# Deformable convolution from weight tables: table writes moved to other queues and paced by patch, loads issued in parts, the image without border columns, tents by a second ACT pass, five product buffers

## The chip, the cores and the metric

The kernel runs on one NeuronCore of a Trainium2 chip, from one launch. The metric is device time in microseconds. TensorE (PE) multiplies matrices, VectorE (DVE) and ScalarE (ACT) work elementwise, GpSimd (POOL) does small jobs, and SyncE (SP) only issues DMAs. SP, ACT and POOL each issue DMAs in the order of their own instruction stream.

## The reference

Two layers on x of shape (8, 128, 64, 64), float32:

```python
# layer 0
v = gn(x)                                   # group norm, 32 groups
om = conv3x3(v, off_w) + off_b              # 27 channels: 18 offsets, 9 masks
# for each of the 9 taps: sample v bilinearly at the tap's place plus its offset,
# times sigmoid(mask); then a sum over taps and channels with w
y = einsum('bckhw,ock->bohw', val, w) + b
x = x + relu(batchnorm(y) * gamma + beta)   # statistics over all 8 images
# layer 1
v = gn(x)
# gate on the pooled v: two of four experts; their 3x3 kernels are mixed per image
x = x + conv3x3(v, mixed) + conv3x3(v, shared_w) + biases
```

## The kernel before, in words

Layer 0 is `dense()`. Offsets here are below 2 in size, so bilinear sampling is written as a product of two tent functions, one along rows and one along columns, each with five shifts (`NR`). A second path, `general()`, is branched over when all offsets are that small.

An image is cut into patches of 8 x 16 pixels, which are the 128 partitions of a matmul. A block is four patches below each other (`t`); an image has eight blocks and 32 patches (`i`). For each patch and each row of taps `ky`:

- `z_part`: one matmul (L425) of the patch's pixels (`xh`) with the weights of three taps gives z in PSUM, and ACT copies it to SBUF (L431). It is emitted one patch ahead.
- `weights`: VectorE multiplies an x tent and a y tent, `x_wts` and `y_wts`, into the product s (L443), one patch ahead, in a pool `ap4` of four buffers.
- `s_part`: three matmuls (L464) of z with s add into `py`, an accumulator with a halo for two patches; `collect` (L481) adds it to the image's half `y` on VectorE. `end_half` takes statistics of y and stores it (L504).

The tents come from two tables per image in DRAM, `y_table` and `x_table` (taby, tabx in the trace). `load_ty` reads the y tents of two patches by eight DMAs on SP into one of three buffers, `load_tx` the x tents of a block by sixteen DMAs on POOL (L393) into one of two buffers. Each broadcasts rows over partitions.

The generator `tables(b + 1)` builds the next image's tables beside the current image. Its steps end in `yield`, and the patch loop calls it: twice after the first tap row, once after the second and third. In order: `repack` of the current image's second half (ACT, L222), loading of x into `pad` (ACT, L243; `pad` is 66 x 66 with zero borders), statistics (VectorE, L257), group norm (a pow on POOL, L277, and ACT, L283), the offset convolution (L310), evacuation twice, once row by row and once column by column (L292, L295), writing both to DRAM (rowwise on ACT, L323; colwise on SP, L327), reading them back with image rows and columns on partitions (`off`, `mask`, on SP, L339 to L341), the sigmoid (L343), the tents (ACT takes absolute values, L348; VectorE clips them, L351, and multiplies by the mask, L352), and the table writes: for each tap and half two y writes on ACT (L360) and one x write on SP (L369). An x write is 64 partitions x 5 shifts x 35 elements of 4 bytes, that is 320 runs of 140 bytes.

`pause(n)` puts n empty yields between steps. The order is written out by hand: each engine runs its instructions in the order of emission. So an instruction that waits holds all behind it on its engine, DMA issues included. Five patches before the image's end what is left of `tables` is emitted at once, and `repack` of the next image follows.

```python
for _ in range(2 if ky == 0 else 1):
    next(made, None)
```

Layer 1 follows (L810 on): per image a residual with gate and an ordinary 3 x 3 convolution (L887). The change does not touch it.

Of the kernel before, what the change touches and what calls it, by code (L numbers as in the profile page):

```python
# [16 lines left out]
P = 128  # L17
# [40 lines left out]
def deform_moe_conv(  # L58
# [122 lines left out]
    def dense():  # L181

        with ExitStack() as st:
# [3 lines left out]
            a3 = st.enter_context(tc.tile_pool(name="d3", bufs=3))  # L187
            ap4 = st.enter_context(tc.tile_pool(name="d4", bufs=4))
            ps_c = st.enter_context(tc.tile_pool(name="ps_c", bufs=2, space=PSUM))
# [4 lines left out]
            nc.gpsimd.memset(zeros, 0.0)  # L194
            pad = padded(a1, "pad")
            offw_sb = a1.tile([P, TAPS, 32], F32, name="offw_sb")
# [20 lines left out]
            def repack(b, h):  # L217

                xh[b, h] = a2.tile([P, NRB // 2, NCB, PC, PR], F32, name="xh")
                for r in range(NRB // 2):  # L220
                    r0 = 1 + PR * (h * NRB // 2 + r)
                    nc.scalar.copy(  # L222
                        xh[b, h][:, r].rearrange("p c x y -> p y c x"),
                        pad[:, r0 : r0 + PR, 1 : W + 1].rearrange("p y (c x) -> p y c x", c=NCB),
                    )
                    yield

            def tables(b):
# [12 lines left out]
                for q in range(4):  # L241
                    rows = slice(16 * q, 16 * q + 16)
                    nc.scalar.dma_start(  # L243
                        out=pad[:, 1 + 16 * q : 17 + 16 * q, 1 : W + 1],
                        in_=x[b].rearrange("c (h w) -> c h w", w=W)[:, rows],
                    )
                if b < 2:
                    for t in tables_of:
                        nc.sync.dma_start(
                            out=t[b].rearrange("(p a n) -> p a n", p=P, n=256),  # L250
                            in_=zeros.unsqueeze(1).to_broadcast([P, fill, 256]),
                        )
                yield from pause(8)
                stats = small.tile([P, NCH, 6], F32, name="stats")
                part = [pad[:, 1 + 8 * c : 9 + 8 * c, 1 : W + 1] for c in range(NCH)]
                for c in range(NCH):
# [45 lines left out]
                for c in range(2):  # L302
                    pc = ps_c.tile([P, CH], F32, name="pc")
                    for k in range(TAPS):
                        ky, kx = divmod(k, 3)
                        if k == LATER and done:
                            evacuate(*done.pop())
                        for j in range(4):
                            r = 16 * j + 8 * c + ky
                            nc.tensor.matmul(  # L310
                                pc[32 * j : 32 * j + 32],
                                lhsT=offw_sb[:, k, :],
                                rhs=pad[:, r : r + 8, kx : kx + W],
                                start=(k == 0),
                                stop=(k == TAPS - 1),
                            )
                        yield
                    done.append((c, pc))
# [3 lines left out]
                for j in range(4):  # L322
                    nc.scalar.dma_start(  # L323
                        out=rowwise[b][:, j * HW // 4 : (j + 1) * HW // 4],
                        in_=omr[32 * j : 32 * j + 27],
                    )
                    nc.sync.dma_start(  # L327
                        out=colwise[b][:, :, H // 4 * j : H // 4 * (j + 1)],
                        in_=omc[32 * j + 9 : 32 * j + 18],
                    )  # L330
                nc.vector.tensor_reduce(
                    most[:, b : b + 1], omr, AX.X, ALU.max, apply_absolute_value=True
                )
                yield from pause(LATER)

                off = a1.tile([P, TAPS, W], F32, name="off")
                mask = a1.tile([H, TAPS, W], F32, name="mask")
                rows = rowwise[b].rearrange("s (h w) -> h s w", w=W)
                nc.sync.dma_start(out=off[0:H], in_=rows[:, 0:9, :])  # L339
                nc.sync.dma_start(out=off[H:P], in_=colwise[b].rearrange("s w h -> w s h"))  # L340
                nc.sync.dma_start(out=mask, in_=rows[:, 18:27, :])  # L341
                yield from pause(LATER)
                nc.scalar.activation(mask, mask, AF.Sigmoid)  # L343
                tent = a1.tile([P, NR, TAPS, W], F32, name="tent", tag="om")
                for i in range(NR + 1):

                    if i < NR:
                        nc.scalar.activation(tent[:, i], off, AF.Abs, bias=steps[:, i : i + 1])  # L348
                    if i:
                        t = tent[:, i - 1]  # L350
                        nc.vector.tensor_scalar(t, t, 1.0, 1.0, ALU.min, ALU.subtract)  # L351
                        nc.vector.tensor_tensor(t[0:H], t[0:H], mask, ALU.mult)  # L352
                    yield
                for k in range(TAPS):
                    ky, kx = divmod(k, 3)
                    for h in range(2):
                        for c in (2 * h, 2 * h + 1):
# [10 lines left out]
                        first = (h * NQI + kx) * NR * HSTEP + (NR - 1) * HSTEP + k * HROWS  # L368
                        nc.sync.dma_start(  # L369
                            out=bass.AP(  # L370
# [14 lines left out]

            def load_tx(t):
                if t >= len(blocks):
                    return
                b, h, c = blocks[t]
                flat = x_wts[t % 2].rearrange("p a b c -> p (a b c)")  # L390
                for qx in range(PC):
                    src = x_table[b][h, PC * c + qx + ROWPAD]
# [4 lines left out]

            def load_ty(u):

# [4 lines left out]
                flat = y_wts[u % 3].rearrange("p j a b c -> p j (a b c)")  # L404
                for qy in range(PR):
                    q = PR * (h * NRB // 2 + r) + qy + ROWPAD
# [89 lines left out]
            def end_half(b, h):  # L496
# [3 lines left out]
                for g in range(first * W // CH, last * W // CH):  # L500
                    at = g * CH - first * W
                    nc.vector.bn_stats(ystats[:, b * NCH + g, :], y[:, at : at + CH])
                    yield
                nc.scalar.dma_start(out=ydram[b][:, first * W : last * W], in_=y)  # L504

# [3 lines left out]
            for _ in tables(0):  # L509
                pass  # L510
            for u in range(2):
                load_ty(u)
                load_tx(u)
            for _ in repack(0, 0):
# [5 lines left out]
            for i, (t, r) in enumerate(patches):  # L520
# [6 lines left out]
                if at == per_image - 5:  # L527
                    for _ in made:
                        pass
                    if b + 1 < B:  # L530
                        made = repack(b + 1, 0)
                if i % 2 == 1:
                    load_ty(i // 2 + 2)
                if r == NRB // 2 - 1:
                    load_tx(t + 2)
                if i % 2 == 0:
                    py = ps_y.tile([P, UR + PR, UC], F32, name="py")
                for ky in range(3):
                    weights(i + 1, ky)
                    s_part(i, ky, py)  # L540
                    z_part(i + 1, ky)
                    for _ in range(2 if ky == 0 else 1):
                        next(made, None)
                    next(ended, None)
# [402 lines left out]
```

## Time and profile before

| what | value |
|---|---|
| median of 3 runs | 2686.2 us (2680.69 to 2688.17) |
| profiled execution, own time | 2694.36 us |
| its span, first to last instruction | 2692.6 us |
| mean granted TensorE clock | 0.897 |
| PE / DVE / ACT / POOL busy | 80% / 58% / 24% / 24% |
| DMA | 355,130 packets, 289.39 MB |
| of these under 512 B | 290,256 packets |

Times in a profile are of one execution. Views used further on: the page with its groups of instructions by line; stretches of the span with the busy time of each engine, the granted clock and the mean busy share of the 16 DMA engines; waits, with what ended them; and the timeline. A name with a small q (SPq, ACTq) is an engine's queue that issues DMAs; "ywts<-taby" is a DMA from the y table into the y tents' buffer. A number in brackets at a timeline row's end is idle time of the engine before it, and what ended it. A gap of an engine that nobody waits for costs nothing.

### The profile page before, as it was taken

How to read it: one execution, taken by the hardware profiler on the slowest of the kernel's cores; microseconds unless marked ns; L12 is line 12 of the kernel's file. 1: busy time of each engine (PE TensorE's matmuls, PEld its weight loads, DVE VectorE, ACT ScalarE, POOL GpSimd, SP SyncE). 2: the span in 40 equal slices, each digit the busy share in tenths (PEclk: the TensorE clock that was granted, in tenths of full speed). 3: DMA queues.
4: the chain of work that ended last, by engine and by line, in shares of the span. 5: the costliest groups of instructions: out<-in, count | busy, mean ns of one | idle time of the engine just before them, and what ended most of it. 6: DMA issues, size and time to landing. Idle time of an engine off the chain costs nothing. (4 is left out here: it accounts for less than half of the span.)

```text
span 2692.6 us, 25651 instructions
## 1 busy us (share of the span) xinstructions
PE 2163.6 (80%) x8530; PEld 1446.2 (54%) x8530; DVE 1550.2 (58%) x1520; ACT 641.0 (24%) x1114; POOL 657.4 (24%) x1141
## 2 busy tenths in 40 slices
PE   3188698759877796689688958895899569999999
PEld 1065575547555665565466636664778424444444
DVE  1075586648665866586577646765798653333321
ACT  2132142213221322132222212221232131111110
POOL 3222132223122322132222222222234142112200
PEclk8599898889898998789798968896999879999999
DMA  3963584396447734873576367635766352222200
GB/s 89 81 161 74 95 168 100 82 103 155 89 87 116 170 70 92 110 159 68 104 119 152 75 90 117 146 75 93 128 149 142 127 181 94 98 94 98 80 34 35
DMA packets 355130, 289.39 MB, mean 107 GB/s; under 512 B 290256, under 2 KB 294352, under 8 KB 353840
## 3 DMA queue, kind: packets, MB, share of 16 engines
q1 hardware_dynamic: 155952, 187.42, 32.2%
q0 software_dynamic: 32768, 56.13, 10.7%
q10 hardware_dynamic: 166272, 44.12, 9.0%
q8 instruction: 71, 1.16, 0.2%
q14 instruction: 67, 0.55, 0.1%
HBM read 231.54 MB, written 55.92 MB: 107 GB/s over the span
## 5 line engine op out<-in xcount | busy, mean ns | idle before, releaser
L443 DVE TENSOR_TENSOR s<-xwts,ywts 128x684 f32<-128x684 f32 (+6 forms) x768 | 1169.4, 1560 | 523.9 <-DMA ywts<-taby 138.2
L464 PE MATMUL py<-s,z 128*128 128x240 f32 (+10 forms) x4608 | 1073.1, 372 | 334.9 <-DVE s L443 239.1
L464 PEld LDWEIGHTS py<-s,z 128*128 128x128 f32 x4608 | 888.2, 203 | 659.8 <-issue 296.2
L393 POOL DMA_DIRECT2D xwts<-tabx x1024 | 526.0, 519 | 1378.3 <-DVE s L443 1114.4
L425 PE MATMUL pz<-dw_sb,xh 128*128 128x384 f32 x1536 | 658.1, 512 | 67.3 <-ACT xh L222 67.3
L431 ACT COPY z<-pz 128x384 f32<-128x384 f32 x768 | 367.5, 481 | 1383.0 <-PE pz L425 1121.6
L887 PE MATMUL pc<-pad,wmix 128*128 128x512 f32 x1152 | 504.1, 598 | 10.7 <-ACT x L826 10.7
L887 PEld LDWEIGHTS pc<-pad,wmix 128*128 128x128 f32 x1152 | 217.2, 190 | 278.1 <-issue 267.4
L425 PEld LDWEIGHTS pz<-dw_sb,xh 128*128 128x128 f32 x1536 | 302.3, 201 | 79.6 <-ACT xh L222 68.2
L895 DVE SCALAR_TENSOR_TENSOR x<-pc,bmix,x 128x512 f32<-128x512 f32 x64 | 47.9, 748 | 321.1 <-PE pc L887 321.1
L310 PE MATMUL pc<-pad,offw_sb 128*32 128x512 f32 x1152 | 155.8, 606 | 9.0 <-ACT pad L283 9.0
L876 ACT ACTIVATE pad<-x,shift,scale 128x512 f32<-128x512 f32 x64 | 51.5, 814 | 329.5 <-PE pc L887 324.8
L827 POOL TENSOR_TENSOR x<-x,xt 128x512 f32<-128x512 f32 x64 | 96.3, 1529 | 54.7 <-ACT x L826 29.4
L481 DVE TENSOR_TENSOR y<-py,y 128x418 f32<-128x418 f32 (+2 forms) x128 | 75.4, 589 | 49.4 <-PE py L464 48.5
L310 PEld LDWEIGHTS pc<-pad,offw_sb 128*32 128x32 f32 x1152 | 32.1, 109 | 96.2 <-issue 72.7
L222 ACT COPY xh<-pad 128x512 f32<-128x512 f32 x64 | 69.5, 1146 | 49.0 <-DMA taby<-tent 49.0
L351 DVE TENSOR_SCALAR tent<-tent 128x576 f32<-128x576 f32 x40 | 17.9, 448 | 97.2 <-ACT tent L348 61.5
L111 POOL TENSOR_TENSOR scale<-ve,nhalf 128x1 f32<-128x1 f32 x8 | 4.4, 547 | 271.2 <-DVE ve L110 271.2
L828 DVE BATCH_NORM_STATS2 stats<-x 128x6 f32<-128x512 f32 x64 | 42.8, 686 | 32.9 <-POOL x L827 25.1
L826 ACT ACTIVATE x<-x,yshift,yscale 128x512 f32<-128x512 f32 x64 | 47.0, 802 | 53.7 <-DMA x<-yd 53.7
L283 ACT ACTIVATE pad<-pad,shift,scale 128x512 f32<-128x512 f32 x64 | 47.6, 809 | 17.1 <-DVE shift L280 17.1
L263 PE MATMUL pm<-mv,gsel 128*128 128x1 f32 x16 | 4.7, 360 | 58.5 <-DVE mv L261 58.5
(85 smaller groups left out, 388.6 us busy)
## 6 DMA issues: line engine op xcount, KB each, us to landing
ywts<-taby SPq DMA_DIRECT2D x1024, 112.5 KB
xwts<-tabx POOLq DMA_DIRECT2D x1024, 53.4 KB, 5.3
pad<-in_x_dram ACTq DMA_DIRECT2D x32, 512.0 KB
xt<-in_x_dram SPq DMA_DIRECT2D x32, 512.0 KB
x<-yd SPq DMA_DIRECT2D x32, 512.0 KB
out_dram<-x SPq DMA_DIRECT2D x64, 256.0 KB
yd<-y ACTq DMA_DIRECT2D x8, 1280.0 KB
tabx<-tent SPq DMA_DIRECT2D x144, 43.8 KB
```

The source lines that it names most:

```text
L222: nc.scalar.copy(xh[b, h][:, r].rearrange("p c x y -> p y c x"), pad[:, r0 : r0 + PR, 1 : W + 1].rearrange("p y (c x) -> p y c x", c=NCB),)
L310: nc.tensor.matmul(pc[32 * j : 32 * j + 32], lhsT=offw_sb[:, k, :], rhs=pad[:, r : r + 8, kx : kx + W], start=(k == 0), stop=(k == TAPS - 1),)
L393: nc.gpsimd.dma_start(out=flat[qx * PR : (qx + 1) * PR, qx * HSTEP : (qx + NR) * HSTEP], in_=src.unsqueeze(0).to_broadcast([PR, NR * HSTEP]),)
L425: nc.tensor.matmul(pz, lhsT=xh[b, h][:, r, c].rearrange("p x y -> p (x y)"), rhs=dw_sb[:, 3 * ky * P : 3 * (ky + 1) * P], start=True, stop ...
L431: nc.scalar.copy(zs[i][:, 3 * ky * P : 3 * (ky + 1) * P], pz)
L443: nc.vector.tensor_tensor(s[:, :, lo:hi, cl:ch], x_wts[t % 2][:, cl:ch, 3 * ky : 3 * ky + 3, first + lo : first + hi].rearrange("p c k r - ...
L464: nc.tensor.matmul(py[:, top + lo : top + hi, cl - kx + 2 : ch - kx + 2], lhsT=zs[i][:, k * P : (k + 1) * P], rhs=s[:, kx, lo:hi, cl:ch], ...
L481: nc.vector.tensor_tensor(part, py[:, rl:rh, cl:ch], part, ALU.add)
L827: nc.gpsimd.tensor_tensor(y, y, xt[:, c % 2 * CH : (c % 2 + 1) * CH], ALU.add)
L876: nc.scalar.activation(pad2[:, 1 + 8 * c : 9 + 8 * c, 1 : W + 1], x1[:, c * CH : (c + 1) * CH].rearrange("p (h w) -> p h w", w=W), AF.Iden ...
L887: nc.tensor.matmul(pc, lhsT=wmix[:, k, :], rhs=pad2[:, 8 * c + ky : 8 * c + ky + 8, kx : kx + W], start=(k == 0), stop=(k == TAPS - 1),)
L895: nc.vector.scalar_tensor_tensor(y, pc, bmix, y, ALU.add, ALU.add)
```

## The change

- `pad` has no border columns (66 rows x 64). Each load is then contiguous per partition. The offset convolution takes the middle taps first; a side tap multiplies 63 of 64 columns.
- A yield follows each of the four loads of x.
- The colwise writes and the three reloads move from SP to ACT; the x table's writes move from SP to POOL. In the patch loop SP issues y loads alone (and, for the first two images, the zero filling of the tables).
- Two waits of `LATER` (4) yields around the reloads become 6, and one of 8 becomes 6. The generator is called three times in an even patch and four times in an odd one, instead of four times in each.
- Tents: ACT takes the absolute value and then relu(1 - t) in a second pass in place; VectorE only multiplies by the mask.
- `load_ty` of a patch pair is issued in two halves of four, in two patches following each other, one patch pair earlier. `load_tx` is issued in parts of 6, 6 and 4 over three patches of the block before.
- `end_half` stores y in pieces of 512 columns.
- The product pool has five buffers instead of four.

```diff
-            ap4 = st.enter_context(tc.tile_pool(name="d4", bufs=4))
+            ap4 = st.enter_context(tc.tile_pool(name="d4", bufs=5))
...
-            pad = padded(a1, "pad")
+            pad = a1.tile([P, HP, W], F32, name="pad")
...
                     nc.scalar.dma_start(
-                        out=pad[:, 1 + 16 * q : 17 + 16 * q, 1 : W + 1],
+                        out=pad[:, 1 + 16 * q : 17 + 16 * q],
                         in_=x[b].rearrange("c (h w) -> c h w", w=W)[:, rows],
                     )
+                    yield
...
-                yield from pause(8)
+                yield from pause(6)
...
-                    for k in range(TAPS):
+                    for n, k in enumerate((1, 4, 7, 0, 3, 6, 2, 5, 8)):
                         ky, kx = divmod(k, 3)
+                        lo, hi = max(0, 1 - kx), min(W, W + 1 - kx)
...
-                                rhs=pad[:, r : r + 8, kx : kx + W],
+                                rhs=pad[:, r : r + 8, lo + kx - 1 : hi + kx - 1],
...
-                    nc.sync.dma_start(
+                    nc.scalar.dma_start(
                         out=colwise[b][:, :, H // 4 * j : H // 4 * (j + 1)],
...
-                yield from pause(LATER)
+                yield from pause(6)
...
-                nc.sync.dma_start(out=off[0:H], in_=rows[:, 0:9, :])
-                nc.sync.dma_start(out=off[H:P], in_=colwise[b].rearrange("s w h -> w s h"))
-                nc.sync.dma_start(out=mask, in_=rows[:, 18:27, :])
-                yield from pause(LATER)
+                nc.scalar.dma_start(out=off[0:H], in_=rows[:, 0:9, :])
+                nc.scalar.dma_start(out=off[H:P], in_=colwise[b].rearrange("s w h -> w s h"))
+                nc.scalar.dma_start(out=mask, in_=rows[:, 18:27, :])
+                yield from pause(6)
...
-                for i in range(NR + 1):
-
-                    if i < NR:
-                        nc.scalar.activation(tent[:, i], off, AF.Abs, bias=steps[:, i : i + 1])
+                for i in range(NR):
+                    t = tent[:, i]
+                    nc.scalar.activation(t, off, AF.Abs, bias=steps[:, i : i + 1])
+                    nc.scalar.activation(t, t, AF.Relu, bias=1.0, scale=-1.0)
                     if i:
-                        t = tent[:, i - 1]
-                        nc.vector.tensor_scalar(t, t, 1.0, 1.0, ALU.min, ALU.subtract)
-                        nc.vector.tensor_tensor(t[0:H], t[0:H], mask, ALU.mult)
+                        t = tent[0:H, i - 1]
+                        nc.vector.tensor_tensor(t, t, mask, ALU.mult)
                     yield
...
-                        nc.sync.dma_start(
+                        nc.gpsimd.dma_start(
                             out=bass.AP(
                                 tensor=x_table[b].tensor,
...
+                    nc.scalar.dma_start(
+                        out=ydram[b][:, g * CH : (g + 1) * CH], in_=y[:, at : at + CH]
+                    )
                     yield
-                nc.scalar.dma_start(out=ydram[b][:, first * W : last * W], in_=y)
...
-            for u in range(2):
-                load_ty(u)
-                load_tx(u)
+            load_tx(0, range(PC))
+            for u in range(3):
+                load_ty(u, range(PR if u < 2 else PR // 2))
...
-                if i % 2 == 1:
-                    load_ty(i // 2 + 2)
-                if r == NRB // 2 - 1:
-                    load_tx(t + 2)
+                load_ty((i + 1) // 2 + 2, range(PR // 2) if i % 2 else range(PR // 2, PR))
+                load_tx(t + 1, range(6 * r, min(PC, 6 * r + 6)))
...
-                    for _ in range(2 if ky == 0 else 1):
+                    next(made, None)
+                    if ky == 0 and i % 2:
                         next(made, None)
```

## The prediction

> **What bounds the kernel now.** I first read the stretches of the dense stage. The starts of the L464 matmuls in the timeline cut it into patches (18 records to a patch, 32 patches to an image). It starts at 131.3 us; images 0 to 6 take 1823.6 us together (260.5 each), image 7 takes 170.5 and layer 1 the last 567.2. Image 7 has no tables to build after it; the others build those of the next image meanwhile.
>
> ```profile
> core 0: us, PE busy (x) PEld busy (x) DVE busy (x) ACT busy (x) POOL busy (x), PEclk, DMA share, GB/s
> 647.00:904.20 257.20, 207.10 (x918) 152.23 (x917) 171.96 (x150) 67.16 (x122) 66.24 (x130) 0.89 0.57 112
> 1954.90:2125.40 170.50, 169.00 (x762) 137.83 (x762) 155.03 (x120) 52.25 (x100) 53.74 (x104) 1.00 0.53 122
> ```
>
> See two things: alone, a pass over an image is bound by TensorE (169.0 of 170.5 us, VectorE close behind with 155.0), and beside the tables TensorE idles 50 us and runs at a lower clock. Next I cut image 2 where its pace changes.
>
> ```profile
> 656.90:692.60 35.70, 23.18 (x76) 17.98 (x75) 22.30 (x24) 4.69 (x10) 8.21 (x16) 0.71 0.81 183
> 704.00:752.20 48.20, 48.20 (x265) 24.48 (x263) 26.71 (x21) 12.53 (x24) 16.47 (x32) 1.00 0.40 76
> 772.60:804.60 32.00, 13.15 (x49) 9.47 (x47) 16.61 (x22) 9.04 (x15) 5.86 (x12) 0.84 0.52 98
> 804.60:862.00 57.40, 38.68 (x144) 30.28 (x145) 28.16 (x22) 8.51 (x18) 12.21 (x24) 0.79 0.67 100
> 862.00:904.20 42.20, 42.19 (x193) 35.12 (x194) 40.67 (x32) 14.74 (x27) 17.48 (x35) 1.00 0.68 151
> ```
>
> These are patches 2-4 (image loading), 7-11 (offset convolution), 16-17 (reload of offsets, tents), 18-23 (tables written) and 24-31. The same patches of image 7 take 16.4, 27.4, 11.9, 31.8 and about 42. So image 2 pays 19.3 + 20.8 + 20.1 + 25.6 + 0 more. The 20.8 is TensorE's own work; the other 65 us are stalls, on no busy engine. The waits of ACT and of SP's queue, then the timeline, say on what.
>
> ```profile
> ACT mask L343 <- DMA mask<-rowwise: 107.3, 8, 14.6
> ACT z L431 <- DMA taby<-tent: 91.0, 31, 5.6
> SPq L407 <- DMA rowwise<-om: 244.9, 8, 37.4
> SPq L407 <- DMA taby<-tent: 218.0, 53, 15.3
> ```
> ```profile
> 783.13 0.68 ACT L343 ACTIVATE mask<-mask 64x576 f32<-64x576 f32 x1 [13.19 <-DMA mask<-rowwise]
> ```
> ```profile
> 804.95 15.94 SPq L407 DMA_DIRECT2D ywts<-taby  x8
> 821.19 7.38 SPq L369 DMA_DIRECT2D tabx<-tent  x8
> 828.68 14.41 SPq L407 DMA_DIRECT2D ywts<-taby  x8
> 843.13 5.26 SPq L369 DMA_DIRECT2D tabx<-tent  x8
> 848.50 7.21 SPq L407 DMA_DIRECT2D ywts<-taby  x8
> ```
> ```profile
> 664.82 4.08 POOL L393 DMA_DIRECT2D xwts<-tabx  x8 [14.40 <-DVE s L443]
> 671.45 0.52 POOL L393 DMA_DIRECT2D xwts<-tabx  x1 [2.56 <-DMA xwts<-tabx]
> ```
>
> ACT stands 13 us before the sigmoid, with the z copies that feed TensorE behind it. SP's y loads stand in turn behind the x table's writes, and VectorE starves. Eight DMAs go out at once, then each waits for one to land: the built program's order has eight completion semaphores for SP and ACT together, and eight for POOL.
>
> **The change, per image (0 to 6).** Floor: image 7's 170.5, plus 20.8 for the convolution (six of nine taps lose 8 of 512 columns, 0.2 us), plus VectorE's extra: 8 statistics x 0.69, 5 mask products x 0.75 and a reduction of 1.2, 10.5 us where it is nearly the bound; the buffers take some, I count 7. The two evacuations lie under the convolution. The five dropped tensor_scalar (0.45 each) give 2.2 that are already out of the 10.5. Floor 198.
>
> Contiguous image: 8,192 packets of 256 B become 512 of 4 KB. The first took 12.2 us of all 16 DMA engines; packets of 4,096 B took 0.2 us elsewhere in this trace, so 6.4 now, spread over four yields. The 10.2 us of VectorE on xwts in patches 2-4 should go. Of the stretch's 19.3, 5.5 are statistics (in the floor); of 13.8 I keep 2. Statistics and normalisation cost the same on contiguous data: 0.69 at L257 against 0.68 at L502, 0.81 at L283 against 0.80 at L826.
>
> Reload and tents: ACT now issues the four colwise writes (0.83 each), the three reloads (1.27, 0.62, 0.63) and five more passes (0.77): 9.7 us, and the y stores as eight DMAs instead of two (about 0.35 each against 0.8, 1 more). ACT's copies fill 1.44 of 5.3 us per patch, so over the five patches 15-20 this fits if it comes in pieces; TensorE runs out after about two copies, 3.5 us. Pauses rise from 4 to 6 at 3.5 yields per patch instead of 4: reloads come 9 us after the writes, the sigmoid 9 after those. Colwise landed 6 us after its last issue (771.1 to 777.2), the mask 5 after its own: the sigmoid's wait goes, the reload may wait some 3 us on ACT. What is late next is the z copy. I keep 4 of 20.1.
>
> Table stage: SP no longer has x writes, so VectorE's wait for y loads goes (they are also issued one patch pair earlier, behind nothing but weights of a patch that VectorE has left; each waits for its buffer, and only y loads queue behind). ACT remains: 7 y writes x 0.63 + 3 copies x 0.48 is 5.9 us per patch against 5.3. And the eight semaphores: before, 16 SP and ACT transfers per patch (8 y writes, 4 x writes, 4 y loads) in 9.6 us mean a turn of 4.8 us; now 11 per patch, 6.6 us at the same turn, 8.3 at 6.0. The same writes in less time load the engines more (0.67 of 57.4 us is 38 us of DMA work), so I take nearer the second: 13 of 5.1 patches' excess (7 to 15). Emission is 91 yields of the 94 there are up to patch 27, so nothing is forced out at once.
>
> POOL: 18 x writes of 320 rows, never seen on POOL here. Price c: its row for 8 rows is 0.52 us, the floor; by packets (320 to that row's 32) 5.2 is the ceiling. SP's row for the very shape is 0.62 against 0.59 for a y load of 32 rows, so the shape hardly counted there; software may count more, and I take 1.0, near the floor. From patch 21 to 27 POOL must do 18c + 20 x 0.52 and wait 5.3 us for the landing: 33.7 of 35.4 us. Cost 2; every microsecond of c above 1.1 costs 18. A gain is excluded: POOL did none of this. The next image needs the tables at patch 31 only. POOL's one pow per image (L277) waits for VectorE with x loads behind it, as before. The fifth product buffer is worth nothing by itself: VectorE's 130 us of waits for a free one happen while TensorE is the bound; it only widens the slack.
>
> Sum: 198 + 2 + 4 + 13 + 2 + 1 for the y stores = 220 against 260.5. Start-up: 36 y writes took 45.7 us sharing semaphores with SP's 18; alone 30 to 45.7, I take 6 off; extra passes add 4, less 2.2: 131.3 becomes 127. Total 127 + 7 x 220 + 170.5 + 567.2 = 2404.7, with the 1.8 us around the span 2406.5. The profiled execution is 8 us over the median of the runs (2694.4 against 2686.2), so about 2400.
>
> **Where the skill weighs in.** SP's issues of x and y loads alternate, with DMA engines 0.67 busy: a queue's order is what is short. The Trainium skill's DMA: Bandwidth & Descriptors (Issuing engines are not separate DMA queues) says DMAs of several issuers share the same 16 engines and spreading saves only issue time. By it the respread is worth nothing and only the contiguous image remains, 7 x 12 us: about 2600. The row differs: the issuer's in-order waits are what VectorE waits for. Second, L393 took 0.52 us beside a nearly always busy VectorE, at most 0.76. SBUF — State Buffer (the box on the "DVE blocks DMA" trap) says VectorE's two-port operations can stretch a GpSimd DMA from about 620 to 3100 ns; at 3.1 the sum would be about 2660.
>
> **Rivals.** Better (0.12): all remaining stalls hidden but 5 us, 203 per image: 2280. For it: 862-904 runs without a stall. ACT in order (0.21): the reload and mask waits stay (13 us) and the turn grows to 8 us, 11 us per patch, 29 us: 245 per image, 2573. For it: ACT's 91 us of waits behind y writes; against it, pauses half as long again. Slower (0.11): POOL's descriptor price. At c = 5.2, 18c + 15.7 is 109 of 35.4 us: 292 per image, and start-up 185 because the tables come through POOL alone: about 2960. It decides from c = 3.3 on (144 us of total per microsecond of c, 286 to lose); at c = 2 the time is 2500. For it: no such row exists; against it: POOL is idle over 70% of an image. No change (0.01): no case aims there. My forecast, 2330 to 2470, has 0.55.
>
> **Numbers.** 2400; the range 2270 to 2620 takes in the better case and nearly all of the ACT rival, leaving out about 0.03 below and 0.16 above. A measurement can tell 0.3% from no change. Faster 0.88, same 0.01, slower 0.11.
>
> **What would show it.** Right: images of 210 to 230 us; no 10 us wait of VectorE for xwts in patches 2-4; ACT's wait at the sigmoid under 3 us; x writes on POOL near 1 us; VectorE's waits for y loads gone; clock above 0.95. Wrong: POOL rows over 2 us with VectorE waiting for xwts at patches 23 and 27; or ACT waiting for landed taby, or colwise, 10 us at a time.

## The result, and the profile after

The changed kernel takes 2727.1 us (median of 4 runs, 2723.9 to 2728.49) against 2684.7 (4 runs, 2680.7 to 2688.2): ratio 1.0157, 95% interval 1.0139 to 1.0175. It is 1.6% slower; 2400 us was forecast, 2270 to 2620 the range. In the profiled execution the span is 2726.7 us, the start-up 132.6, images 0 to 6 take 1851.4 (before 1823.6), image 7 173.2 and layer 1 569.6. Lines have moved: the product s is L456 (was L443), its matmul L477 (L464), z L438 and its copy L444, x loads L406, y loads L420, x writes L382, y writes L373, the sigmoid L354, the image loads L246, the y stores L516.

The stretches of the changed kernel's trace answer to those of before: image 2, image 7, then of image 2 the patches 1-4 (image loading), 9-15 (convolution), 16-20 (reload, tents), 21-26 (tables written) and 27-31.

```profile
core 0: us, PE busy (x) PEld busy (x) DVE busy (x) ACT busy (x) POOL busy (x), PEclk, DMA share, GB/s
652.60:918.80 266.20, 205.16 (x917) 151.12 (x916) 168.33 (x144) 70.21 (x127) 77.19 (x148) 0.87 0.57 108
1983.90:2157.20 173.30, 169.79 (x763) 140.90 (x761) 151.92 (x118) 52.42 (x100) 50.20 (x101) 0.98 0.56 125
657.30:688.30 31.00, 23.74 (x98) 19.51 (x97) 21.81 (x21) 8.43 (x16) 6.63 (x14) 0.83 0.75 204
717.70:777.00 59.30, 58.68 (x313) 32.61 (x312) 33.23 (x25) 14.53 (x28) 17.24 (x35) 1.00 0.35 68
777.00:810.70 33.70, 28.03 (x121) 22.93 (x120) 28.53 (x27) 14.59 (x26) 6.51 (x14) 0.90 0.61 147
810.70:893.00 82.30, 39.38 (x144) 30.81 (x143) 33.04 (x26) 9.43 (x20) 22.57 (x39) 0.73 0.65 82
893.00:918.80 25.80, 25.80 (x123) 21.55 (x122) 22.25 (x18) 10.91 (x19) 13.31 (x28) 1.00 0.59 114
```

The row to see is 810.70:893.00: six patches in 82.3 us with no engine busy even half of the time, the clock at 0.73. There the change lost more than it had won elsewhere. Cutting every image at the starts of the py matmuls gives patch times; these are their sums in us, as means over images 1 to 6, beside image 7 of the changed kernel (excess is after less image 7):

```
patches                   before   after   image 7   forecast as excess   excess found
0-4    image loading        44.6    34.0     25.4*        2                    8.6
5-8    statistics           29.6    30.2     21.7         (in the floor)       8.5
9-14   convolution          45.3    54.2     31.9         20.8                22.4
15-20  reload, tents        70.3    39.5     31.2         4 + products         8.4
21-26  tables written       46.9    82.8     32.9         13 (+2 POOL)        49.9
27-31                       25.4    25.3     23.6         0                    1.8
sum                        262.1   266.1    166.6
* not stalled, as in e5 below; image 7 itself took 32.0 here, for the y stores of image 6
```

(Rows are by patch number. Before, the convolution lay in patches 7-11 and the table writes in 18-23, so in its column 29.6 and 45.3 share the one, 70.3 and 46.9 the other. Its patches 18-23 took 60.6 us: against these the table stage, now 82.8, lost some 22 us an image.) What the waits say, first SP's queue over the whole run, then the first of these waits within the patch loop alone (133 to 2157 us), then ACT, then the product's group before and after, and the x writes:

```profile
SPq L420 <- DMA taby<-tent: 498.3, 88, 100.9
...
SPq L420 <- DMA yd<-y: 153.1, 25, 17.8
```
```profile
SPq L420 <- DMA taby<-tent: 397.4, 87, 26.0
```
```profile
ACT z L444 <- DMA taby<-tent: 64.9, 35, 4.2
...
ACT mask L354 <- DMA mask<-rowwise: 0.9, 1, 0.9
```
```profile
L443 DVE TENSOR_TENSOR s<-xwts,ywts 128x684 f32<-128x684 f32 (+6 forms) x768 | 1169.4, 1560 | 523.9 <-DMA ywts<-taby 138.2
```
```profile
L456 DVE TENSOR_TENSOR s<-xwts,ywts 128x684 f32<-128x684 f32 (+6 forms) x768 | 1159.3, 1559 | 510.6 <-DMA ywts<-taby 312.3
...
L382 POOL DMA_DIRECT2D tabx<-tent x144 | 97.9, 685 | 141.0 <-ACT tent L359 77.1
```

ACT's wait at the sigmoid, 107.3 us before, is 0.9. An x write costs POOL 0.685 us. But VectorE's wait for y loads rose from 138.2 to 312.3 us (62.4 of it before the first patch), and SP's y loads, now alone on SP in the patch loop, wait 498.3 us for *landed y-table writes* (218.0 before). Of the 498.3, 100.9 are one wait at start-up, for the first table itself; the 397.4 in the loop (202.6 before) are all in patches 21, 23 and 25. The timeline shows the place, and a stretch inside it what was busy:

```profile
814.81 2.62 ACTq L373 DMA_DIRECT2D taby<-tent  x4
817.82 1.26 ACTq L373 DMA_DIRECT2D taby<-tent  x2
...
820.91 2.66 POOL L382 DMA_DIRECT2D tabx<-tent  x4 [0.80 <-DMA tabx<-tent]
838.22 3.17 DVE L456 TENSOR_TENSOR s<-xwts,ywts 128x720 f32<-128x720 f32 x2 [23.44 <-DMA ywts<-taby]
840.00 1.54 PE L477 MATMUL py<-s,z 128*128 128x240 f32 x3 [23.51 <-DVE s L456]
```
```profile
820.00:838.00 18.00, 0.00 (x0) 0.00 (x0) 0.00 (x0) 0.00 (x0) 2.77 (x5) 0.50 0.99 61
```

VectorE stands 23.44 us. Taken apart by single DMA and completion semaphore (the built program hands eight of them round among SP's and ACT's DMAs), this is one patch pair's eight y loads. A packet bears no load's name; last bytes here and below are found by counting a table's packets off in order of their ends, 32 to a y load and 8 to an x load.

```
y loads 1-6 of the pair   issued 797.05 to 800.89
y load 7                  issued 821.15; its semaphore was last that of a y write on ACT,
                          issued 814.81, landed 821.14
y load 8                  issued 823.80; likewise: y write issued 816.13, landed 823.78
y load 7                  last byte 827.01, semaphore seen 835.13
y load 8                  last byte 829.67; VectorE starts 838.22
```

Two things in one stall. Load 7 stands 20 us for a write that was issued 14 us after load 6: the order in which a semaphore passes from DMA to DMA is fixed when the program is built, and a load can be placed in it behind a write of another queue that is issued much later. And then 8.5 us pass from the last byte to VectorE's start, where another pair of this image needed 1.2 (last byte 667.0, start 668.2).

### The profile page after: what moved, and what is told of

The parts are those of the page before. It is cut to its first block, busy times and chain, and to the rows that moved or that the text cites. A ratio compares the mean times of both kernels' runs of the same rounds, so it can differ in the third digit from the quotient of the medians.

```text
span 2726.7 us, 25525 instructions
## 1 busy us (share of the span) xinstructions
PE 2136.3 (78%) x8530; PEld 1429.9 (52%) x8530; DVE 1522.7 (56%) x1480; ACT 666.3 (24%) x1154; POOL 742.6 (27%) x1283
## 5 line engine op out<-in xcount | busy, mean ns | idle before, releaser
L456 DVE TENSOR_TENSOR s<-xwts,ywts 128x684 f32<-128x684 f32 (+6 forms) x768 | 1159.3, 1559 | 510.6 <-DMA ywts<-taby 312.3
L477 PE MATMUL py<-s,z 128*128 128x240 f32 (+10 forms) x4608 | 1061.7, 369 | 389.2 <-DVE s L456 345.5
L477 PEld LDWEIGHTS py<-s,z 128*128 128x128 f32 x4608 | 882.0, 201 | 703.0 <-issue 410.4
L406 POOL DMA_DIRECT2D xwts<-tabx x1024 | 509.3, 503 | 1202.2 <-DVE s L456 1034.2
L444 ACT COPY z<-pz 128x384 f32<-128x384 f32 x768 | 366.9, 480 | 1427.7 <-PE pz L438 1307.9
L438 PE MATMUL pz<-dw_sb,xh 128*128 128x384 f32 x1536 | 648.1, 505 | 69.6 <-ACT xh L225 69.6
L438 PEld LDWEIGHTS pz<-dw_sb,xh 128*128 128x128 f32 x1536 | 298.2, 199 | 82.9 <-ACT xh L225 70.5
L318 PE MATMUL pc<-pad,offw_sb 128*32 128x504 f32 (+1 forms) x1152 | 157.3, 599 | 19.3 <-ACT pad L289 19.3
L382 POOL DMA_DIRECT2D tabx<-tent x144 | 97.9, 685 | 141.0 <-ACT tent L359 77.1
L301 DVE TENSOR_SCALAR om<-pc,offb_sb 128x512 f32<-128x512 f32 x16 | 12.0, 751 | 86.6 <-ACT om L298 86.6
```

The lines of the kernel that those rows point to most:

```text
L318: nc.tensor.matmul(pc[32 * j : 32 * j + 32].rearrange("p (h w) -> p h w", w=W)[:, :, lo:hi], lhsT=offw_sb[:, k, :], rhs=pad[:, r : r + 8, ...
L382: nc.gpsimd.dma_start(out=bass.AP(tensor=x_table[b].tensor, offset=x_table[b].offset + first + (0 if h else ROWPAD), ap=[[NR * HSTEP, W], ...
L406: nc.gpsimd.dma_start(out=flat[qx * PR : (qx + 1) * PR, qx * HSTEP : (qx + NR) * HSTEP], in_=src.unsqueeze(0).to_broadcast([PR, NR * HSTEP]),)
L438: nc.tensor.matmul(pz, lhsT=xh[b, h][:, r, c].rearrange("p x y -> p (x y)"), rhs=dw_sb[:, 3 * ky * P : 3 * (ky + 1) * P], start=True, stop ...
L444: nc.scalar.copy(zs[i][:, 3 * ky * P : 3 * (ky + 1) * P], pz)
L456: nc.vector.tensor_tensor(s[:, :, lo:hi, cl:ch], x_wts[t % 2][:, cl:ch, 3 * ky : 3 * ky + 3, first + lo : first + hi].rearrange("p c k r - ...
```

## The experiments

Two theories were stated. **S**: a y load on SP waits for a completion semaphore whose last user stands in ACT's own order. **W**: landings are held up while many small table writes are in flight. Further rivals appear in the expectations. Every kernel is the changed one with the edit shown; a ratio is to the kernel before on the same chip. e1, e2, e3 and e5 ran beside a before of 2687.25 us, e4 and e6 to e11 beside 2733.99, e12 and e13 beside 2729.9. All but the last two are single runs, and seven runs of before on the last chip spread over 2719 to 2743, so single ratios closer than about 0.005 are not told apart. Expected times were worked out on the changed kernel's 2727 us beside a before of 2685, so on the other chips the ratios are to be compared, or the patches. "Patches" are means over images 1 to 6. On the chip of e4 and e6 to e11 an untouched table stage takes 87.9 (e6) and 87.5 (e8) in patches 21-26, against 82.8 in the changed kernel's trace.

**e1_xwrites_sync.** The x writes back on SP.

```diff
-                        nc.gpsimd.dma_start(   # x_table write
+                        nc.sync.dma_start(
```

> The changed kernel with one part undone: the x table's writes are issued by SP again, not by POOL. The changed kernel takes 2727 us; its images 1 to 6 take 266 us, of which about 50 us are stalls in patches 21 to 26, where the tables are written. Theory S (completion semaphores): SP and ACT take turns at eight of them; a y load then holds one that a y write of ACT held before, and that write stands behind z copies, which wait for TensorE, for VectorE and so for the y load before. By S, x writes on SP do not help: they stand in front of y loads and take the same eight, so the stalls stay between 25 (kernel before) and 50 us: 2640 to 2760. Theory W (landing): the small writes from POOL, beside those of ACT, hold up every landing (14 us instead of 4 for a y load); by W they fall to 15 to 25 us, 2500 to 2560.

Measured: 2672.65 us, ratio 0.9946. Patches 21-26 take 59.9 instead of 82.8, patches 27-31 39.8 instead of 25.3. So the move that the forecast counted on most, x writes off SP, costs 2% by itself. W's number is missed by more than 110 us; S's range holds it.

**e2_no_xwrites.** No x writes for images 2 to 7.

```diff
-                        nc.gpsimd.dma_start(   # x_table write
+                        b < 2 and nc.gpsimd.dma_start(
```

> The changed kernel without the x table's writes for images 2 to 7 (their x table is an older one, so only images 0 and 1 sample by their own offsets). Image 0 of the loop still writes and is the control. Theory W (POOL's small writes hold up the landings): images 1 to 6 lose most of their 50 us of stalls in patches 21 to 26, to 15 or less each, 2727 - 6 x 35 = about 2515. Theory S (shared completion semaphores of SP and ACT): POOL's writes use eight others, so 35 or more of the 50 us stay: 2640 or more.

Measured: 2623.49, ratio 0.976. Patches 21-26 fall from 82.8 to 64.7: 18 of the 49.9 us go, 32 stay; image 0, whose pass still writes both tables, takes 73.8 (73.2 in the changed kernel). S's 2640 or more is missed by 17 us, W's 2515 by 108: neither theory alone. The gain lies in patch 21 (28.7 to 12.8), where VectorE waits for y loads only, so it does not come from POOL's own queue:

```profile
810.77 1.63 DVE L456 TENSOR_TENSOR s<-xwts,ywts 128x720 f32<-128x720 f32 x1 [6.39 <-DMA ywts<-taby]
```

The x writes share no semaphore with the y loads, and still hold them up: that is W.

**e3_no_ywrites.** No y writes for images 2 to 7.

```diff
-                            nc.scalar.dma_start(   # y_table write
+                            b < 2 and nc.scalar.dma_start(
```

> The changed kernel without the y table's writes for images 2 to 7 (their y table is an older one). The x writes from POOL stay. Theory S: with no y write of ACT ahead of them on a shared semaphore, y loads of patches 21 to 26 are never late: stalls of 50 us fall below 10 in images 1 to 6, about 2727 - 6 x 42 = 2475. Theory W: the x writes still hold up landings, half or more of the 50 us stays, 2580 or more.

Measured: 2528.35, ratio 0.941. Patches 21-26 take 35.6, 2.7 over image 7's: the stall is the y writes' (image 0, which still writes them, keeps 74.7). The total is above S's figure because patches 27-31 rose to 38.5 with POOL's x loads behind its x writes; in image 2, patch 27:

```profile
825.08 4.62 DVE L456 TENSOR_TENSOR s<-xwts,ywts 128x684 f32<-128x684 f32 x3 [18.47 <-DMA xwts<-tabx]
```

**e5_ywrites_pool.** The y writes on POOL too; nothing left out.

```diff
-                            nc.scalar.dma_start(   # y_table write
+                            nc.gpsimd.dma_start(
```

> The changed kernel with the y table's writes on POOL too: POOL issues all 54 table writes of an image, and they use its own eight semaphores, while SP and ACT keep theirs for y loads, image, offsets and y stores. POOL has 54 x 0.69 + 20 x 0.50 = 47 us to issue over the six patches of 5.3 us. Theory S: y loads are no longer late; x loads are, by about 15 us; stalls of 15 to 25 us in patches 21 to 27 instead of 50, 2500 to 2560. Theory W: the same small writes, now all from POOL, hold up the landings at least as much: 2700 or more.

Measured: 2611.22, ratio 0.9717. With the same bytes in flight as in the changed kernel, patches 21 and 22 take 5.8 and 5.7 (36.2 together in the changed kernel): W as the main cause falls, since it asked for 2700 or more. Patches 0-4 take only 25.4, though the y stores stay on ACT. In image 2 all sixteen y loads of the next two pairs took semaphores that other y loads had used last, where in the changed kernel the seventh stands behind a y store: with fewer DMAs in it, the turn fell differently. That is luck, and no merit of the move. The miss of S's number is new: 54 writes on POOL delay the x loads, so that patch 23 takes 17.3 us and patch 27 28.2. In image 2, patch 27:

```profile
858.65 4.62 DVE L456 TENSOR_TENSOR s<-xwts,ywts 128x684 f32<-128x684 f32 x3 [32.97 <-DMA xwts<-tabx]
```

**e4_y_late.** y loads issued eight at a time and one patch pair later, as in the kernel before.

```diff
-                load_ty((i + 1) // 2 + 2, range(PR // 2) if i % 2 else range(PR // 2, PR))
+                if i % 2 == 1:
+                    load_ty(i // 2 + 2, range(PR))
```

> The changed kernel with the y loads emitted as before: all eight of a patch pair at once, one patch pair later. Theory S (a y load holds a completion semaphore after a y write of ACT): the loads come still later and with less time in hand, the stalls of patches 21 to 26 stay at 50 us or grow, 2720 to 2800. Rival E: the early issue does the damage (loads waiting for VectorE to leave their buffer hold SP and semaphores); then the stalls fall to 25 us as in the kernel before, 2550 or less.

Measured: 2771.49, ratio 1.0137, patches 21-26 88.2, as in e6 and e8 on the same chip. When the y loads are issued makes no difference that can be told; a load that stands behind another queue's write stands there early or late.

**e6_one_ystore.** Each half of y stored by one DMA instead of pieces.

```diff
-                    nc.scalar.dma_start(
-                        out=ydram[b][:, g * CH : (g + 1) * CH], in_=y[:, at : at + CH]
-                    )
                     yield
+                nc.scalar.dma_start(out=ydram[b][:, first * W : last * W], in_=y)
```

> The changed kernel with one y store per half image again, instead of pieces of 512 columns. SP's y loads waited 153 us in all for y stores. Theory S: patches 1 and 2 lose their stall of about 9 us per image, 2727 - 7 x 9 = 2664. If the stall has another cause (x loads, the repack), nothing moves: 2727.

Measured: 2777.63, ratio 1.016, where S's 2664 is a ratio of 0.992. The stall of patch 1 is gone (11.6 to 5.2) and stands in patches 3 and 4 instead (14.2 and 7.1): no gain.

**e7_ywrites_sp.** The y writes on SP, behind the y loads that are emitted before them; x writes stay on POOL.

```diff
-                            nc.scalar.dma_start(   # y_table write
+                            nc.sync.dma_start(
```

> The changed kernel with the y table's writes on SP, where the y loads are; x writes stay on POOL. The writes use the same eight semaphores as before, but no longer stand behind ACT's z copies. Theory S1 (it is ACT's order that holds them): SP has 7 writes and 4 loads of 0.6 us per patch, 6.6 us against 5.3, so stalls of 8 to 20 us instead of 50: 2430 to 2520 with the rest unchanged. Theory S2 (eight in flight are too few, whoever issues): 35 us or more stay, 2620 or more.

Measured: 2592.78, ratio 0.948; patches 21-26 take 42.2 instead of 82.8 (87.5 to 88.2 on the same chip). This is the plainest test of S: the same loads and writes, the same eight semaphores, but one queue, on which no load is placed behind a write that is issued later. In size it lies between the two forms of S: S1's range is a ratio of 0.905 to 0.939, S2's 0.976 or more. The move also frees ACT of issuing 36 writes an image, as e3 and e5 do; that it is the semaphores' order that counts is read from the stall above, in which VectorE waits for two loads and SP for two y writes, and not for ACT's copies. SP's waits in the trace of e7 (total us, times, longest), and the last of them within its patch loop (138 to 2020 us), now read:

```profile
SPq L420 <- DMA yd<-y: 138.0, 26, 17.5
...
SPq L373 <- DMA taby<-tent: 102.0, 66, 7.4
SPq L420 <- DMA taby<-tent: 75.9, 56, 5.6
```
```profile
SPq L420 <- DMA taby<-tent: 73.8, 55, 5.6
```

The y loads' 397.4 us behind y writes in the loop have become 73.8. What is left moved to patches 25-27 (10.5, 7.1, 19.3); e7's timeline and stretches there:

```profile
822.21 9.75 SPq L420 DMA_DIRECT2D ywts<-taby  x4
...
833.31 3.94 POOL L406 DMA_DIRECT2D xwts<-tabx  x8 [10.21 <-DMA tabx<-tent]
...
838.26 4.62 DVE L456 TENSOR_TENSOR s<-xwts,ywts 128x684 f32<-128x684 f32 x3 [18.76 <-DMA taby<-tent]
```
```profile
775.65:820.74 45.09, 36.41 (x146) 28.86 (x145) 32.39 (x25) 9.39 (x20) 20.18 (x34) 0.89 0.89 81
820.74:840.00 19.26, 5.14 (x25) 4.02 (x24) 1.74 (x2) 5.55 (x8) 7.34 (x16) 0.70 1.06 86
```

The DMA share (the column before GB/s; it sums the packets' own times, so it can pass 1) is 0.89 and then 1.06, at only 81 to 86 GB/s, while image 7 of the changed kernel has 0.56 at 125 GB/s. With the order out of the way it is landings that set the end: in patch 25 of this image the last y load of the pair was issued at 797.2 and had its last byte at 809.2, one microsecond before VectorE went on. (The name in the timeline's last bracket is that of a DMA that uses the same semaphore; VectorE waits there for the pair's y loads, issued up to 831.43, and the new block's x tents.)

**e8_pm_later.** The statistics' small matmul three steps later.

```diff
                 nc.vector.bn_aggr(mv, stats)
+                yield from pause(3)
                 pm = ps_s.tile([P, 4], F32, name="pm", tag="pss")
...
-                yield from pause(LATER)
+                yield from pause(1)
```

> The changed kernel with TensorE's group mean matmul (the one behind the aggregated statistics) emitted three yields later and the pause after it cut by three. Patch 5 takes 13.9 us against 5.6 in image 7. Theory M: TensorE, in order, waits there for VectorE's statistics behind its products; then patch 5 falls to 6 to 8 us, 2727 - 7 x 6 = 2685. Rival V: VectorE's 5.5 us of statistics are the cost wherever the matmul stands: 2715 to 2727.

Measured: 2760.27, ratio 1.0096, just under V's range (1.011 to 1.016 as a ratio) and far from M's 1.000. Patch 5 falls from 13.9 to 6.0 and patch 6 rises from 5.8 to 12.0: patches 5-8 together 28.9 instead of 30.2. The stall goes with the step; the matmul's place is not its cause, or only for a microsecond.

**e9_ystores_pool.** e7 with the y stores on POOL.

```diff
-                    nc.scalar.dma_start(   # y store, ydram
+                    nc.gpsimd.dma_start(
```

> The changed kernel with two streams moved: the y-table writes to SP (as in e7_ywrites_sp) and, new, the eight y stores of each image (L516) from ACT to POOL, so that neither shares a completion semaphore with ACT's own order. Theory S (a y load on SP waits for a semaphore whose last user stands in ACT's order): the stall in patches 1 and 2 is the same as that in 21 to 26, with y stores in the place of y writes; 12.6 + 7.5 us in e7 against a floor of 5.2 each falls under 12 together, 8 to 10 us less per image over 7 images, a ratio to the kernel before of 0.918 to 0.928 (e7 had 0.948). Rival (the load of the next image, four transfers of 512 rows in the same patches, fills the DMA engines and holds the y loads up whoever issues the y stores): patches 1 and 2 stay at 17 or more and the ratio at 0.94 or more.

Measured: 2579.84, ratio 0.9436, against e7's 0.948: the expected 0.918 to 0.928 is missed. Patch 1 is down from 12.6 to 5.2 and patch 2 from 7.5 to 5.6, as S said; but 3 and 4 rise to 12.4 and 7.1. The waits of SP's queue between 624 and 662 us of e9, and then its timeline:

```profile
SPq L420 <- DMA pad<-in_x_dram: 18.5, 3, 16.7
```
```profile
637.68 24.33 SPq L420 DMA_DIRECT2D ywts<-taby  x23
...
649.91 3.98 DVE L456 TENSOR_TENSOR s<-xwts,ywts 128x660 f32<-128x660 f32 x3 [8.57 <-DMA ywts<-taby]
```

The y loads now wait for landed image loads, which share the semaphores too.

**e10_and_no_xwrites.** e9 without the x writes of images 2 to 7.

```diff
-                        nc.gpsimd.dma_start(   # x_table write
+                        b < 2 and nc.gpsimd.dma_start(
```

> e9_ystores_pool without the x-table writes for images 2 to 7 (images 0 and 1 still write both tables; the later ones read stale x tables). Left out: those 18 writes per image. Theory W (small writes in flight hold up the landing of everything else): with y and x writes both flying, patches 25 to 27 took 10.5 + 7.1 + 19.3 us in e7 against about 16 of floor; without the x writes they fall under 24, and six images give 13 to 20 us each, a ratio 0.03 to 0.045 below e9's. Rival (the x writes cost only POOL's queue or nothing, SP's own y writes and y loads in one order are what holds patches 25 to 27): they stay at 32 or more, and the ratio within 0.01 of e9's.

Measured: 2428.62, ratio 0.888, 0.055 below e9, more than the 0.045 at most that W asked for. Patches 25 to 27 take 5.6, 5.6 and 5.3 instead of 10.2, 6.9 and 18.0; over 21-31 the x writes cost 21.7 us per image (86.1 to 64.4). So W is real, as what comes second: about a third of the changed kernel's stall goes with the x writes (18 of 49.9 in e2), and all of what e9 has left in patches 25 to 27. In patch 27 part of it may be POOL's own order, since x loads wait there for landed x writes (10.21 us in the row of e7) and e10 takes this away too; only patch 21 of e2 shows W by itself.

**e11_spread.** e9, with the same writes starting earlier and lying further apart.

```diff
-                yield from pause(6)      # twice, around the reloads
+                yield from pause(4)
...
                         yield
+                    if k < 7:
+                        yield
```

> e9_ystores_pool with the same table writes spread over more patches: both pauses before the tents are 4 steps instead of 6, and each of seven taps gets one step more, so that the writes start about one patch earlier and take about seven patches instead of five. Theory W with a rate (36 y and 18 x writes of 320 short runs are about 38 us of work for the DMA engines, by 0.67 of 57.4 us in the kernel before, pressed into 5 patches of 5.3 us, 27 us): spreading leaves less in flight at a time, patches 25 to 27 fall by 8 to 16 us, ratio 0.02 to 0.04 below e9's. Rival (each write costs a fixed stall in SP's order, wherever it stands): the stall moves with the writes, the sum of patches 20 to 27 stays within 4 us, ratio within 0.01 of e9's. Either way the shorter pauses may bring back up to 5 us at the sigmoid (patches 15 to 20, 39.5 us in e7).

Measured: 2571.6, ratio 0.9406. Patches 25 to 27 fall from 35.1 to 22.2 us, inside the 8 to 16 expected; patch 23 takes 13.5 instead of 7.9, and the shorter pauses give 3.4 back in patches 15-20. Patches 20 to 27 fall by 4.4 in all (66.6 to 62.2), near the rival's 4, and the net 0.3% is not told apart from nothing. That the DMA engines' work for 54 writes is the same wherever it lies would fit, but is not shown.

**e12_image_pool.** e11 with the image loads on POOL.

```diff
-                    nc.scalar.dma_start(   # pad <- x
+                    nc.gpsimd.dma_start(
```

> e11_spread with the four image loads (L246) issued by POOL instead of ACT; nothing else. In e9 and e11 the stall left patches 1 and 2 and came back in 3 and 4 (12.2 + 7.2 us, floor 5.2 each), with SP's y loads waiting 16.7 us for a landed image load. Theory S (shared semaphores): with the image loads among POOL's eight semaphores the y loads are free, patches 3 and 4 fall under 12 together, 7 to 9 us less per image, ratio 0.02 below e11's 0.941, 0.915 to 0.925; SP's wait for the image's landing is gone. Rival (the image's 2 MB fill the DMA engines, so y loads land late whatever they wait for): 3 and 4 keep 17 or more and the ratio stays within 0.005 of e11's. A cost may appear under either: POOL's x loads now share semaphores with the image loads, and patches 2 to 4 could wait for xwts, up to 10 us per image.

Measured: 2570.3 (4 runs), ratio 0.9434, interval 0.938 to 0.949: no gain, patches 3 and 4 take 11.0 and 7.6. The total looks like the rival's, but its trace gives the third answer of the expectation:

```profile
633.92 0.53 POOL L246 DMA_DIRECT2D pad<-in_x_dram  x1 [0.54 <-PE py L479]
634.45 0.52 POOL L408 DMA_DIRECT2D xwts<-tabx  x1
...
638.34 1.50 POOL L408 DMA_DIRECT2D xwts<-tabx  x3 [3.38 <-issue]
...
649.14 3.98 DVE L458 TENSOR_TENSOR s<-xwts,ywts 128x660 f32<-128x660 f32 x3 [7.58 <-DMA ywts<-taby]
```

The releaser in the last bracket is misnamed. The y loads of that patch pair had their last byte at 634.5, 14.6 us earlier. The last four x loads of the new block, the four shown, were issued behind image loads on POOL at 634.45 to 639.35 and had their last bytes at 644.2 to 647.2, two microseconds before VectorE starts (the last one's semaphore was full at 648.57, and VectorE's wait for that semaphore ended at 648.61); in e9 those four were complete at 636.6 and the y loads only at 646.1. The image loads changed queue, and with it their victim. That patches 3 and 4 need not stall is shown by e5, where the y loads of that pair were issued 7 us and more before the first image load. What the busy DMA engines (DMA share 0.92 in 617.0 to 638.7 of e12) add to each landing is not separated.

**e13_spread_timed.** e11 again, timed.

> e11_spread once more, timed in three rounds beside the kernel before: the version with y writes on SP, y stores on POOL, and the table writes spread. One look gave a ratio of 0.941; every theory expects 0.935 to 0.947 and an interval wholly below 0.96, so that the changed kernel's parts are worth 5 to 6.5 per cent once the y loads share no semaphore with transfers in ACT's order. If the interval reached 0.96 the single looks would have been disturbed.

Measured: 2565.7 (2564.4 to 2574.3, 4 runs) against 2729.9, ratio 0.9408, interval 0.936 to 0.946. The version with y writes on SP, y stores on POOL and spread writes beats both kernels: 6% faster than before, and 7% below the changed kernel by the two ratios.

## Why the prediction was wrong

**The floor** held. The convolution was priced at 20.8 us, and patches 9-14 pay 22.4. Patches 27-31 are free of stalls, as said.

**Image loading** held in the step that was priced: VectorE's wait for x tents in patches 2-4 is gone, and patches 0-4 fell from 44.6 to 34.0. Of 13.8 I kept 2; 8.6 are left, and they are new: patches 1 and 2, where y loads wait for landed y stores (most of the 153.1 us on SP's queue; in image 2 the seventh y load of a pair stands from 643.5 to 660.9 for a store issued at 655.99). I had priced the eight y stores as ACT issues, 1 us, and not as users of shared semaphores.

**Statistics**: about 5.5 us in the floor, 8.5 found; e8 only moves it by one patch.

**Reload and tents** held: 4 us plus the mask products (3.75, in the floor) were forecast, 8.4 found, and ACT's wait at the sigmoid went from 107.3 to 0.9. Start-up is 132.6, not 127.

**The table stage is the step that failed.** It had 13 us for the eight semaphores, said that without x writes on SP "VectorE's wait for y loads goes", and that SP's y loads would stand "behind nothing but weights of a patch that VectorE has left". VectorE's wait for y loads rose instead, and 49.9 were found: 37 too many in each image, some 258 over seven, of the 322 by which the span exceeds the 2404.7 of the sum. The semaphores had been seen, but counted as a rate, so many transfers per turn, and only against ACT's writes. What decides is who stands ahead of whom: a load on SP that takes its semaphore after a y write on ACT waits until ACT has come to that write and the write has landed. Moving the x writes away did not free the y loads. With the x writes back on SP the stage costs 59.9 (e1), with the y writes on SP as well as the loads 42.2 (e7). About a third of the stall (18 of 49.9, e2) goes with the x writes, by W: writes pressed into less time hold up the landings of all else, which I had only as a turn of 6.0 instead of 4.8 us.

**The rivals.** POOL's price (0.11, the only slower case) did not come: an x write took 0.685 us, below the 1.0 taken and far from 3.3, and an x load 0.503 beside VectorE, at most 0.77. "ACT in order" (0.21) named the right queue with the wrong victim: ACT's z copies wait only 64.9 us for y writes in all, while SP's loads wait 397.4 in the loop for the same writes. Its price, 29 us, was 20 short. The slower side was thus given to a mechanism that could not reach it.

**Issue time or order.** By the Trainium skill's DMA: Bandwidth & Descriptors (Issuing engines are not separate DMA queues), spreading over issuers saves only issue time; I set it aside for a gain. Measured, the choice of issuer is worth more than issue time, and in both directions: one group of writes moved from ACT to SP, with nothing else changed, takes the ratio to the kernel before from 1.0157 to 0.948 (e7); x writes moved from SP to POOL take it from 0.9946 (e1) to 1.0157. The same page (Queues, rings and completion order) says that a semaphore's increment lands only after every earlier write of that DMA engine, across its queues. That would fit the 8.1 us between load 7's last byte and its semaphore while table writes were in flight; no run here isolates it.

**Open**: why patches 5-8 pay 8.5 us, and how the late landings of W divide between full DMA engines and late completion signals.

## What to carry to other kernels

Before moving DMAs to another queue, list for each load on the critical path which transfer last used its completion semaphore, on which engine that transfer is issued, and when that engine comes to it; a load is only as early as the latest of these. Writes that stand behind compute belong either on the queue of the loads that an engine waits for, emitted after them, or among other semaphores. When a stall goes, follow it to the next transfer in the same turn before counting the gain: e6 and e9 removed one and got it back two patches later, and e12 only changed its victim.

## What the runs showed of the hardware, not expected

A y load's semaphore was seen 8.1 us after its last byte (827.01 to 835.13) while x and y writes were flying; elsewhere VectorE started 1.2 us after the last byte. While table writes of 320 short runs went out, the DMA share was 0.89 to 1.06 at 81 to 86 GB/s (e7), and 0.99 at 61 GB/s in the changed kernel's stall. And 320 runs of 140 bytes cost POOL 0.685 us to issue, against 0.503 for its x loads.
